# One-hot matrices kept in bf16 for the later layers of a graph network, with changes to its first and last steps

## The chip, the cores and the metric

One core of a Trainium2 chip runs the whole kernel. Its engines have an instruction stream each: TensorE (PE in the profile, its weight loads PEld) multiplies matrices, VectorE (DVE) and ScalarE (ACT) work on elements, GpSimd (POOL) issues the gathers, SyncE (SP) issues plain DMAs. All DMAs share 16 DMA engines. The metric is the device time of one execution in microseconds (us). Three runs of the kernel before gave 2895.53, 2903.81 and 2903.98 us, a median of 2903.81 us.

## The reference, cut to what matters

There are n = 6250 nodes with D = 256 features and 100000 edges, sorted by their target `dst`. `src` is random, and each edge has one of three relation types and 32 attributes.

```
ew = edge_attr @ edge_w + edge_b                    # one weight row per edge
rel_masks = [(edge_type == i) for i in range(3)]
inv_cnt = [1 / max(segment_sum(m, dst, n), 1) for m in rel_masks]
for l in range(3):
    msg = relu(x[src] * ew)
    out = sum over i of (segment_sum(msg * rel_masks[i], dst, n) * inv_cnt[i]) @ weights[l, i]
    x = x + relu(out + x @ roots[l] + biases[l])
result = layernorm(x_input + x)
```

## The kernel before, in words

**Tiles, pairs, quads and steps.** 128 edges are a tile, two tiles a pair, two pairs a quad; there are 782 tiles, 391 pairs and 196 quads. A layer is a loop over steps `it`, and at step `it` the pair `order[it]` is reduced. The parts of a pair's work stand in the same loop at different distances ahead of the reduction: the gather 9 steps ahead (`AHEAD`), the edge weights 6 to 4, the weighing 3, the one-hots 2. Every engine takes its instructions in the order in which this loop writes them (a manual schedule), and what one engine needs of another it waits for by semaphore. The planner (`order_of`, `spans_of`, `stages`, `schedule`) works out in which order the pairs come, which pairs form a span (pairs whose targets lie within 40 neighbouring nodes), at which step a span's sums are added, and at which step a block of 128 nodes is finished (`starts`). Layer 0 has 391 steps, layers 1 and 2 have 414 each.

**One pair.** `gather_pair` (L1378) has POOL fetch 128 rows of x for each tile, by an indirect DMA; the rows of a quad go to one of `ROWS` = 8 buffers `xs`. In layer 0 PE makes the edge weights out of the attributes and `ew_sb` (`make_ew`, L811 for the bias and L815), ACT copies them to `keep` (`keep_ew`, L771), and SP stores them in `ew_all` (L772). In layers 1 and 2 SP loads them again (`load_ew`, L759) and ACT copies them to PSUM (`seed_ew`, L786). DVE multiplies the rows by them (`weigh`, L838), ACT applies the relu (L839). `one_hot` makes the matrix that says which node of the window, and which relation, an edge belongs to: on DVE four `tensor_scalar` a quad (L852, one a tile, 128 x 120 in float32), in all three layers; in layer 0 ACT also writes a bf16 copy `oh_b` (L855), used to count edges. PE multiplies rows and one-hot (`reduce`, L870 and L878) into PSUM, for a span of several pairs the sums are turned (`take`, `turn`), and DVE adds them to `acc` (`add`, L918).

**The zone.** The first 52 pairs (few nodes, many edges) are gathered in layer 0 only: their rows are sorted by source class (`sort_hot`, `sort_count` with L628 to L632) and scattered by POOL to `zone_table` (`scatter`, L733) once their weights are in `keep`. Layers 1 and 2 load them in 39 lots (`load_ew`, L754) and make their one-hots from what was loaded.

**Nodes.** `node_mul` (L947, PE) multiplies a block's sums by the weights, `node_end` (DVE, L978 and L981) scales, adds and applies the relu, and SP stores the block in `x_mid` (L984). A block `c` has `node_mul` part 0 at step `starts[c]`, `node_end` part 0 and `node_mul` part 1 two steps later, `node_end` part 1 and the store four steps later; `clear` then empties its place in `acc`. In layer 2 `deviate` and `norm` follow.

**From layer to layer.** The next layer's first six pairs (12 gathers, `gather_early`) are fetched from all of `x_mid` but node block 1, so POOL waits at the first of them for the last store of the other 48 blocks. Block 1 is finished last of all; the gathers of the seventh pair on read the whole of `x_mid` and need its store too.

**The beginning.** The first part (`look`) reads `dst`, finds windows and sets `flag`; behind it a branch opens `ordered_path`, which loads `edge_w` and `edge_b` (L490 to L498), splits the bias into three bf16 parts (L505 to L511), zeroes `acc` in three large writes (L524 to L529), and stores a row block of zeros in each `x_mid` (L534). Then layer 0 begins. At step 20 of layer 0 `find_rows` and `find_came` prepare the indices of the later layers.

Of the kernel before, what the change touches and what calls it, by code (L numbers as in the profile page):

```python
# [442 lines left out]
def ordered_path(ctx, tc, x, attr_laid, A, weights, roots, biases, edge_w, edge_b, out, src, src_i, seg, place_i, consts, x_root,  # L443
# [7 lines left out]
    P = 128  # L451
# [30 lines left out]
    ew_all = [dram.tile([P, 4 * D], F32, name=f"ew_all{q}") for q in range(-(-U // 2))]  # L482
    table = dram.tile([(classes + 2 * Z) * P, D + 2], F32, name="zone_table")
# [4 lines left out]
    ew_sb = early_pool.tile([P, 2, D], F32, name="ew_sb")  # L488
    nc.vector.memset(ew_sb, 0.0)
    for j in range(OCT):  # L490
        nc.scalar.dma_start(ew_sb[j * A:(j + 1) * A, j % 2, :], edge_w)
    seed = early_pool.tile([P, D], F32, name="seed")
    nc.scalar.dma_start(seed, edge_b[None, :].to_broadcast([P, D]))
    blank = early_pool.tile([P, D + 2], F32, name="blank")
    bias = blank.bitcast(BF)[:PARTS, :2 * D].rearrange("p (i d) -> p i d", i=2)
    with tc.tile_pool(name="bias_s", bufs=1) as bias_s:
        left = bias_s.tile([P, D], F32, name="left")
        nc.scalar.dma_start(left, edge_b[None, :].to_broadcast([P, D]))  # L498
        row = bias_s.tile([P, 1], F32, name="row")
        nc.vector.tensor_copy(row, node_i)  # L500
        is_row = bias_s.tile([P, PARTS], F32, name="is_row")
        part = bias_s.tile([P, D], BF, name="part")
        rows_of = bias_s.tile([P, D], F32, name="rows_of")
        nc.vector.memset(rows_of, 0.0)
        for k in range(PARTS):  # L505
            nc.vector.tensor_scalar(is_row[:, k:k + 1], row, float(k), None, op0=ALU.is_equal)
            nc.vector.tensor_copy(part, left)
            nc.vector.tensor_sub(left, left, part)
            nc.vector.scalar_tensor_tensor(rows_of, part, is_row[:, k:k + 1], rows_of, op0=ALU.mult, op1=ALU.add)
        for i in range(2):  # L510
            nc.vector.tensor_copy(bias[:, i, :], rows_of[:PARTS, :])  # L511

# [20 lines left out]
    for rows_of in x_mid:  # L533
        nc.scalar.dma_start(rows_of[N - P:N, :], x_all[:, NT - 1, :])  # L534
# [47 lines left out]
    hots = {}  # L582
# [41 lines left out]
    def sort_count(g):  # L624
        n, t = len(tiles_in(g)), 3 * g
        seat = o_pool.tile([P, 2, D], F32, name="o_p")
        flat = seat.rearrange("p a d -> p (a d)")[:, :n * classes]
        nc.tensor.matmul(flat, before, hots[g][:, :n].rearrange("p t w -> p (t w)"), start=True, stop=False)  # L628
        nc.tensor.matmul(flat, full_ones, total[:, :n].rearrange("p t w -> p (t w)"), start=False, stop=True)
        nc.vector.tensor_mul(hots[g][:, :n], flat.rearrange("p (t w) -> p t w", w=classes), hots[g][:, :n])  # L630
# [23 lines left out]
    def sort_step(it):  # L654
# [30 lines left out]
    def layer(l, r_sb, b_sb, ats, early, pools):  # L685
# [6 lines left out]
        soon = min(SOON, steps - max(starts[:1] + starts[2:]) - 5)  # L692
# [10 lines left out]
        at_qs = {}  # L703
# [143 lines left out]
        def one_hot(q):  # L847
# [5 lines left out]
            if l == 0:  # L853
                oh_bs[q] = early_pool.tile([P, 4, WK], BF, name="oh_b", bufs=2)
                nc.scalar.activation(oh_bs[q][:, :n], ohs[q][:, :n], AF.Copy)  # L855
# [710 lines left out]
```

## Time and profile before

| | |
|---|---|
| median of three runs | 2903.81 us (2895.53 to 2903.98) |
| the profiled execution, its own time | 2903.96 us |
| its span, first to last instruction | 2902.2 us |
| mean granted TensorE clock | 0.948 |
| first gather begins | 4.04 us |
| first gather for layer 1 begins | 1159.06 us |
| first gather for layer 2 begins | 2017.61 us |
| last gather begins | 2882.09 us |
| DMA traffic | 668.25 MB, mean 230 GB/s |

How to read its rows: in a timeline each row has the start and the duration in us, engine, line, operation, what is written and read, and in brackets how long the engine had been idle before and what released it ("issue" is time in which the engine waited for nothing that the profile shows). A group's row has the count, busy us and the mean ns of one, then the idle time before. A row of waits has the sum in us, the number of times and the longest. A row of windows has the stretch and, for each engine, the busy us and the number of instructions.

### The profile page before, as it was taken

The numbers are of one execution on the slowest core, as the hardware profiler recorded it, in microseconds if no ns is written. First come the engines' busy times: TensorE is split into PE (matmuls) and PEld (weight loads), VectorE is DVE, ScalarE is ACT, GpSimd is POOL, SyncE is SP. The second block draws the span as 40 slices with busy tenths as digits, with TensorE's granted clock in tenths as the row PEclk, the third lists the DMA queues.
The fourth block names the chain that finished last, engine by engine and source line by source line (L and its number), as shares of the span: only waits on it lengthen the run. The fifth ranks groups of instructions, "written<-read, shape, count | busy, mean of one in ns | idle before, by whom it ended". The sixth has DMA issues, their size and how long they took to land. (4 is left out here: it accounts for less than half of the span.)

```text
span 2902.2 us, 44132 instructions
## 1 busy us (share of the span) xinstructions
PE 2409.1 (83%) x13302; PEld 1880.6 (65%) x13302; DVE 2207.5 (76%) x5612; ACT 1708.1 (59%) x2220; POOL 2138.6 (74%) x2253
## 2 busy tenths in 40 slices
PE   5799988888988789788898888777888888878776
PEld 2466656555666566577777777665666767767665
DVE  7777766766656576677878888776788888888986
ACT  5677766666666667455655555444555555555654
POOL 7676777777777775777777777776777777767775
PEclk9899998999889999999999999898999999999998
DMA  7898665556555666887777777676777777777765
GB/s 237 280 328 272 207 198 190 189 185 196 185 192 187 196 211 202 267 262 240 256 242 243 246 237 257 215 223 195 269 255 262 255 256 240 244 227 233 249 227 156
DMA packets 285411, 668.25 MB, mean 230 GB/s; under 512 B 50555, under 2 KB 142509, under 8 KB 285165
## 3 DMA queue, kind: packets, MB, share of 16 engines
q1 hardware_dynamic: 170112, 362.98, 35.9%
q0 software_dynamic: 107616, 294.11, 33.9%
q10 hardware_dynamic: 7436, 8.24, 0.9%
q8 instruction: 110, 1.80, 0.3%
q14 instruction: 137, 1.11, 0.1%
HBM read 528.50 MB, written 136.63 MB: 229 GB/s over the span
## 5 line engine op out<-in xcount | busy, mean ns | idle before, releaser
L1378 POOL DMA_INDIRECT xs<-x_mid,src_r x1332 | 1265.3, 950 | 420.1 <-issue 343.1
L1378 POOL DMA_INDIRECT xs<-in_x_dram,src_io x770 | 734.9, 954 | 243.1 <-issue 211.8
L839 ACT ACTIVATE xs<-xs 128x1024 f32<-128x1024 f32 x533 | 559.5, 1050 | 582.8 <-DVE xs L838 561.0
L838 DVE TENSOR_TENSOR xs<-ew_p,xs 128x1024 f32<-128x1024 f32 x533 | 646.5, 1213 | 314.3 <-ACT keep L771 176.3
L878 PE MATMUL h_p<-oh,xs 128*128 128x120 f32 x4768 | 692.5, 293 | 202.7 <-DVE acc L918 105.4
L878 PEld LDWEIGHTS h_p<-oh,xs 128*128 128x128 f32 x4768 | 641.3, 203 | 304.9 <-DVE acc L918 112.4
L852 DVE TENSOR_SCALAR oh<-iota_w,seg_o 128x120 f32<-128x120 f32 x2138 | 568.2, 328 | 0.0
L870 PE MATMUL h_p<-xs,oh 128*120 128x256 f32 x1868 | 517.7, 405 | 41.5 <-issue 14.7
L947 PE MATMUL o_p<-w_sb,acc 128*128 128x256 f32 (+1 forms) x1752 | 456.1, 397 | 64.8 <-DVE x_root L978 56.6
L918 DVE TENSOR_TENSOR acc<-h_p,acc 128x240 f32 (+1 forms) x764 | 338.9, 445 | 113.5 <-PE o_p L947 45.7
L947 PEld LDWEIGHTS o_p<-w_sb,acc 128*128 128x128 f32 (+1 forms) x1752 | 323.6, 195 | 141.5 <-DVE x_root L978 73.9
L870 PEld LDWEIGHTS h_p<-xs,oh 128*120 128x120 f32 x1868 | 319.5, 189 | 146.6 <-issue 30.0
L786 ACT ACTIVATE ew_p<-ew_s 128x1024 f32<-128x1024 f32 (+1 forms) x340 | 343.3, 1010 | 12.7 <-DMA ew_s<-ew_all 12.7
L771 ACT ACTIVATE keep<-ew_p 128x1024 f32<-128x1024 f32 x170 | 173.2, 1019 | 226.1 <-issue 115.5
L978 DVE SCALAR_TENSOR_TENSOR x_root<-o_p,inv,x_root 128x256 f32<-128x256 f32 (+1 forms) x438 | 210.5, 480 | 43.0 <-PE o_p L947 36.1
L839 ACT ACTIVATE zone<-zone 128x1024 f32<-128x1024 f32 (+1 forms) x78 | 78.8, 1010 | 223.9 <-DVE zone L838 223.9
L815 PE MATMUL ew_p<-ew_sb,at 64*128 64x512 f32 x630 | 199.0, 710 | 11.8 <-ACT ew_p L789 11.7
L789 ACT ACTIVATE ew_p<-seed 128x1024 f32<-128x1024 f32 (+1 forms) x194 | 198.5, 1023 | 0.0
L931 PE MATMUL r_p<-r_sb,t_s 128*128 128x256 f32 x588 | 158.7, 392 | 21.7 <-ACT t_s L927 21.4
L838 DVE TENSOR_TENSOR zone<-ew_p,zone 128x1024 f32<-128x1024 f32 (+1 forms) x78 | 90.6, 1162 | 107.5 <-PE ew_p L801 107.3
L870 PE MATMUL h_p<-zone,oh 128*120 128x256 f32 x576 | 148.0, 387 | 11.6 <-DVE acc L918 7.0
L801 PE MATMUL ew_p<-x_all,hot 128*128 128x256 f32 x588 | 150.6, 401 | 7.6 <-DVE hot L794 7.4
(178 smaller groups left out, 2340.8 us busy)
## 6 DMA issues: line engine op xcount, KB each, us to landing
ew_s<-ew_all SPq DMA_DIRECT2D x338, 512.0 KB
ew_all<-keep SPq DMA_DIRECT2D x169, 512.0 KB
zone<-zone_table SPq DMA_DIRECT2D x72, 516.0 KB
xs<-x_mid,src_r POOLq DMA_INDIRECT x1332
zone_table<-blank SPq DMA_DIRECT2D x21, 677.2 KB
xs<-in_x_dram,src_io POOLq DMA_INDIRECT x770
x_mid<-x_all SPq DMA_DIRECT2D x96, 128.0 KB
at<-in_attr_laid_dram SPq DMA_DIRECT2D x40, 256.0 KB
```

The costliest lines, as they stand in the source:

```text
L786: nc.scalar.activation(ew_ps[q][:, :n], ew_ss[q][:, :n], AF.Copy)
L789: nc.scalar.activation(ew_ps[q][:, :n], seed[:, None, None, :].to_broadcast([P, n, 2, D]), AF.Copy)
L815: nc.tensor.matmul(ew_ps[q][:, k].rearrange("p i d -> p (i d)"), at[half, :], ew_sb[half].rearrange("p i d -> p (i d)"), start=False, stop ...
L838: nc.vector.tensor_mul(there, ew_ps[q][:, pairs.start:pairs.stop, :n], there)
L839: nc.scalar.activation(there, there, AF.Relu)
L852: nc.vector.tensor_scalar(ohs[q][:, i, :], iota_w[:, :, :WIN], at, None, op0=ALU.is_equal)
L870: nc.tensor.matmul(h_p[:WK, :D], ohs[u // 2][:, t, :], rows_of(u, i), start=(i == 0 and first), stop=(i == n - 1 and closes(u)), skip_grou ...
L878: nc.tensor.matmul(h_p[:, d * WK:(d + 1) * WK], rows_of(u, i)[:, d * P:(d + 1) * P] if d < DC else full_ones, (ohs if d < DC else oh_bs)[u ...
L918: nc.vector.tensor_tensor(there, h_ps[span][:, :CH * WK].rearrange("p (c r w) -> p c r w", c=CH, r=R), there, op=ALU.add)
L947: nc.tensor.matmul(o_p[:n, j, :], acc[:, d, r, slot:slot + n], w_sb[:, r * DC + d, :], start=(d == 0), stop=(d == DC - 1))
L978: nc.vector.scalar_tensor_tensor(root, o_p[:n, j, :], inv[:n, c, r:r + 1], root, op0=ALU.mult, op1=ALU.add)
L1378: nc.gpsimd.indirect_dma_start(out=xs[:, u % 2, i, :], out_offset=None, in_=x_rows[:, :], in_offset=bass.IndirectOffsetOnAxis(ap=src_i[:, ...
```

## The change

- **One-hots.** In layer 0 SP stores each regular quad's bf16 one-hots (`oh_b`, now three buffers) in a new DRAM tensor `oh_all`, 128 rows of 960 bytes. In layers 1 and 2 SP loads them six steps ahead (`load_oh`, three buffers), and ACT widens them to float32 in one instruction a quad, in the place of the four DVE instructions. The zone's lots keep theirs.
- **The sort.** What DVE does with the counts (`sort_rank`) moves one step behind the PE multiplications (`sort_count`), and the sorting steps may lie one step closer to the node steps.
- **The beginning.** `edge_b` and `edge_w` are loaded ahead of the look instead of behind the branch, into four places of `x_root` (`staged`; `ROOTS` is 21, and layer 0 uses 17); the bias is split at the end of the look. The copies of window bases in the look are grouped by equal span length: 16 in place of 54. `acc` is zeroed by ACT alone: 256 columns before layer 0, the rest in nine pieces at steps 0, 2, ... 16. The zero rows of `x_mid` are stored by SP instead of ACT.
- **The last steps.** The last five blocks (`QUICK`) have their parts one step apart in place of two; their starts in layer 0 become 366, 369, 372, 375, 378 (before: 366, 370, 374, 378, 382), in layers 1 and 2 388, 392, 396, 399, 402 (before: 388, 393, 397, 401, 405). The span that ends with the last pair is added as soon as it is summed, and the very last span has five pairs in place of seven. The number of steps and the start of block 1 stay.

```
+    oh_all = [dram.tile([P, 4 * WK], BF, name=f"oh_all{q}") for q in range(-(-U // 2))]
...
+    ew_sb, bias, seed = staged(x_root)
...
-    for c in range(DC + 1):
-        if c < DC // 2:
-            nc.vector.memset(acc[:, c], 0.0)
-        else:
-            nc.scalar.activation(acc[:, c].rearrange("p r n -> p (r n)"),
-                                 zero.to_broadcast([P, R * (ASIDE + 2 * P + WIN)]), AF.Copy)
+    def zero_acc(n0, n1):
+        nc.scalar.activation(acc[:, :, :, n0:n1], zero[:, :, None, None].to_broadcast([P, DC + 1, R, n1 - n0]), AF.Copy)
+
+    zero_acc(P, 3 * P)
+    zero_at = {0: (3 * P, 4 * P), 2: (ASIDE, ASIDE + P), 4: (ASIDE + P, ASIDE + 2 * P + WIN), 6: (4 * P, 5 * P),
+               8: (5 * P, 6 * P), 10: (6 * P, 7 * P), 12: (7 * P, 8 * P), 14: (0, P), 16: (RING, ASIDE)}
...
     for rows_of in x_mid:
-        nc.scalar.dma_start(rows_of[N - P:N, :], x_all[:, NT - 1, :])
+        nc.sync.dma_start(rows_of[N - P:N, :], x_all[:, NT - 1, :])
...
-                           if not any(s - 1 <= p <= s + 4 for s in taken_by)))
+                           if not any(s <= p <= s + 4 for s in taken_by)))
...
+    def sort_rank(g):
+        n, t = len(tiles_in(g)), 3 * g
+        flat = seats[g].rearrange("p a d -> p (a d)")[:, :n * classes]
         nc.vector.tensor_mul(hots[g][:, :n], flat.rearrange("p (t w) -> p t w", w=classes), hots[g][:, :n])
...
         if it in sort_at[:-1]:
             sort_count(sort_at.index(it))
+        if it - 1 in sort_at[:-1]:
+            sort_rank(sort_at.index(it - 1))
...
+        def load_oh(q):
+            n = tiles_of(q)
+            oh_ls[q] = late_pool.tile([P, 4, WK], BF, name="oh_l", bufs=3)
+            nc.sync.dma_start(oh_ls[q][:, :n].rearrange("p t w -> p (t w)"), oh_all[q][:, :n * WK])
...
         def one_hot(q):
             ohs[q] = edge.tile([P, 4, WK], F32, name="oh", bufs=3)
             n = tiles_of(q)
+            if q in oh_ls:
+                nc.scalar.activation(ohs[q][:, :n], oh_ls[q][:, :n], AF.Copy)
+                return
...
-                oh_bs[q] = early_pool.tile([P, 4, WK], BF, name="oh_b", bufs=2)
+                oh_bs[q] = early_pool.tile([P, 4, WK], BF, name="oh_b", bufs=3)
                 nc.scalar.activation(oh_bs[q][:, :n], ohs[q][:, :n], AF.Copy)
+                if 2 * q >= Z:
+                    nc.sync.dma_start(oh_all[q][:, :n * WK], oh_bs[q][:, :n].rearrange("p t w -> p (t w)"))
...
+        next_at = {s + paces(c, NT): c for s, c in node_at.items()}
+        over_at = {s + 2 * paces(c, NT): c for s, c in node_at.items()}
...
+            if l > 0 and pair(LOAD_OH) is not None and first_of(it + LOAD_OH, 2) and pair(LOAD_OH) < ZU:
+                load_oh(pair(LOAD_OH) // 2)
             if l > 0 and pair(LOAD_EW) is not None and first_of(it + LOAD_EW, 2):
                 load_ew(pair(LOAD_EW) // 2)
...
+            if l == 0 and it in zero_at:
+                zero_acc(*zero_at[it])
...
-            if it - 2 in node_at:
-                node_end(node_at[it - 2], 0)
-            if it - 4 in node_at:
-                node_end(node_at[it - 4], 1)
+            if it in next_at:
+                node_end(next_at[it], 0)
+            if it in over_at:
+                node_end(over_at[it], 1)
...
-    stops = {K, last, middle, *quads, *lots}
+    stops = {K, last, last + 5, middle, *quads, *lots}
...
+        if spans[group[-1]][1] == -(-E // 256):
+            by = 0
         by = max(by, done + 1 + some)
...
+def paces(c, NT):
+
+    return 1 if c >= NT - QUICK else 2
...
-        step = starts[c] = max(done[c] + 2, step + 4)
+        step = starts[c] = max(done[c] + paces(c, NT), step + 2 + paces(max(c - 1, 2), NT))
...
+def staged(x_root):
+    D = x_root.shape[2]
+    first = ROOTS - STAGED
+    return (x_root[:, first:first + 2, :],
+            x_root.bitcast(BF)[:PARTS, first + 2, :].rearrange("p (i d) -> p i d", i=2),
+            x_root[:, first + 3, :])
...
+        ew_sb, bias, seed = staged(x_root)
+        A = edge_w.shape[0]
+        nc.scalar.dma_start(seed, edge_b[None, :].to_broadcast([P, D]))
+        nc.vector.memset(ew_sb, 0.0)
+        for j in range(OCT):
+            nc.scalar.dma_start(ew_sb[j * A:(j + 1) * A, j % 2, :], edge_w)
...
+        left = look.tile([P, D], F32, name="left")
+        is_row = look.tile([P, PARTS], F32, name="is_row")
+        part = look.tile([P, D], BF, name="part")
+        rows_of = look.tile([P, D], F32, name="rows_of")
+        for k in range(PARTS):
+            rest_of = left if k else seed
```

More of the change, by code (lines that the diff above doesn't have):

```diff
@@ L487, in ordered_path @@
     early_pool = only.enter_context(tc.tile_pool(name="first", bufs=1, side="right"))
[L488 to L493, printed above, removed]
-    blank = early_pool.tile([P, D + 2], F32, name="blank")
[L495 to L511, printed above, removed]
+    ew_sb, bias, seed = staged(x_root)
+    blank = early_pool.tile([P, D + 2], F32, name="blank")
     x_all = big.tile([P, NT, D], F32, name="x_all")
@@ L691, in layer @@
         steps = len(order)
-        soon = min(SOON, steps - max(starts[:1] + starts[2:]) - 5)
+        soon = min(SOON, steps - starts[0] - 5, *(steps - starts[c] - 2 * paces(c, NT) - 1 for c in range(2, NT)))
         taken, turns, added, banks = stages(N, E, share, l)
@@ L1459 @@
             nc.vector.tensor_scalar(limits[:, 0, last:clear], limits[:, 0, last:clear], float(P), None, op0=ALU.max)
+        runs = []
         for u, v in spans_of(N, E)[Z // 2:]:
-            if v > u + 1:
-                nc.vector.tensor_copy(base_g[:, u + 1:v], base[:, u:u + 1].to_broadcast([1, v - u - 1]))
+            if runs and runs[-1][1] == v - u:
+                runs[-1][2] += 1
+            else:
+                runs.append([u, v - u, 1])
+        for u, n, k in runs:
+            if n > 1:
+                there = base_g[:, u:u + n * k].rearrange("p (k n) -> p k n", n=n)
+                first = base[:, u:u + n * k].rearrange("p (k n) -> p k n", n=n)[:, :, 0:1]
+                nc.vector.tensor_copy(there[:, :, 1:], first.to_broadcast([1, k, n - 1]))
         base_p = look_p.tile([P, 512], F32, name="base_p", bufs=1)
```

49 lines of the change are left out of this document (31 added, 18 removed).

## The prediction

> **What bounds the kernel now.** I read the page first, then the groups by line, then POOL's timeline from end to end, and last the waits and windows of the stretches where POOL stops. No engine is full on the page, and the busiest, PE and DVE, suggest that moving DVE's work is worth much:
>
> ```profile
> span 2902.2 us, 44132 instructions
> PE 2409.1 (83%) x13302; PEld 1880.6 (65%) x13302; DVE 2207.5 (76%) x5612; ACT 1708.1 (59%) x2220; POOL 2138.6 (74%) x2253
> q1 hardware_dynamic: 170112, 362.98, 35.9%
> ```
>
> POOL's 74% misleads. Its groups of gathers and scatters:
>
> ```profile
> L1378 POOL DMA_INDIRECT xs<-x_mid,src_r x1332 | 1265.3, 950 | 420.1 <-issue 343.1 <-DMA xs<-x_mid,src_r 15.2 <-ACT xs L839 12.6
> L1378 POOL DMA_INDIRECT xs<-in_x_dram,src_io x770 | 734.9, 954 | 243.1 <-issue 211.8 <-DMA xs<-in_x_dram,src_io 6.1 <-PE ew_p L815 5.2
> L733 POOL DMA_INDIRECT zone_table<-keep,slot_i x104 | 101.9, 980 | 42.9 <-issue 25.9 <-ACT keep L765 11.5 <-DMA xs<-in_x_dram,src_io 2.7
> ```
>
> A gather is busy for 0.95 us, and the timeline puts 0.30 us of "issue" behind each, so one takes 1.25 us and a pair 2.5 us. With the 36 gathers that open the layers these are 2242, about 2802 us of a span of 2902. POOL's timeline has only these larger holes:
>
> ```profile
> 4.04 1.11 POOL L1378 DMA_INDIRECT x_root<-in_x_dram,src_f  x1 [1.67 <-DMA src_f<-in_src_laid_dram]
> ...
> 94.16 0.95 POOL L1378 DMA_INDIRECT xs<-in_x_dram,src_io  x1 [0.30 <-issue]
> ...
> 105.04 0.94 POOL L1378 DMA_INDIRECT xs<-in_x_dram,src_io  x1 [7.43 <-issue]
> ...
> 293.82 1.00 POOL L733 DMA_INDIRECT zone_table<-keep,slot_i  x1 [11.48 <-ACT keep L765]
> ...
> 1159.06 0.94 POOL L1378 DMA_INDIRECT xs<-x_mid,src_e  x1 [16.81 <-DMA x_mid<-x_all]
> ...
> 1174.06 0.94 POOL L1378 DMA_INDIRECT xs<-x_mid,src_r  x1 [0.30 <-issue]
> ...
> 2017.61 0.95 POOL L1378 DMA_INDIRECT xs<-x_mid,src_e  x1 [9.23 <-issue]
> ...
> 2450.54 0.94 POOL L1378 DMA_INDIRECT xs<-x_mid,src_r  x1 [1.03 <-issue]
> ...
> 2619.78 1.11 POOL L1378 DMA_INDIRECT xs<-x_mid,src_r  x1 [2.27 <-ACT xs L839]
> ...
> 2882.09 0.95 POOL L1378 DMA_INDIRECT xs<-x_mid,src_r  x1 [0.30 <-issue]
> ```
>
> Beyond the usual 0.30 us they are: 7.1 us at 105; 11.2 at 294; 16.5 at 1159; 8.9 at 2018; twelve between 2450 and 2620 (first and last shown) with 14.3 in sum; three small ones before 290 with 1.5. Together 59.5 us. Everything else is gathers, the first 4.0 us, and 20.1 us from the last gather's start to the end. So POOL sets the pace nearly everywhere, and I count only what the change does to these holes and to the two ends. Cheaper DVE work where POOL does not stop is worth nothing.
>
> **The first stretch, to 294 us.** Here the steps run behind POOL, and POOL stops at 105 because its eight buffers are full and at 294 because the first scatter needs weights that ACT has not yet copied. If the steps come d earlier at 294, POOL goes on d earlier, up to the 19.8 us of the five holes. Four edits move d:
>
> ```profile
> 30.94 1.01 PE L811 MATMUL ew_p<-blank,full_ones 3*128 3x512 bf16 x2 [14.67 <-DVE blank L511]
> 0.74 0.40 SPq L1425 DMA_DIRECT2D src_f<-in_src_laid_dram  x1
> 18.83 3.67 SPq L563 DMA_DIRECT2D at<-in_attr_laid_dram  x2
> 5.88 3.54 DVE L1462 COPY base_g<-base 1x5 f32<-1x5 f32 x54
> 20.49 0.48 DVE L489 MEMSET ew_sb<- 128x512 f32 x1
> 26.71 0.29 DVE L507 CAST part<-left 128x256 bf16<-128x256 f32 x1 [0.90 <-DMA left<-in_L_gnn_edge_b_dram]
> 30.35 0.54 DVE L511 CAST blank<-rows_of 3x256 bf16<-3x256 f32 x2
> 1114.38 1.15 ACT L964 ACTIVATE acc<-zero_o 128x1152 f32<-128x1152 f32 x1
> 145.10:217.60 72.50, 67.53 (x359) 45.31 (x359) 56.78 (x152) 54.90 (x74) 54.45 (x58) 1.00 0.97 328
> DVE sort_hot L630 <- PE o_p L629: 13.0, 11, 3.0
> ```
>
> (1) PE's first edge weights wait for the bias until 30.94. With the bias split ahead of the branch only DVE's `full_ones` is left. DVE passed the branch at 20.49; the look gains the bias work (first and last row: 26.71 to 30.89, 4.2 us) and a 0.48 us zeroing, and loses some 2.5 of the 3.54 us of copies (16 in place of 54), so `full_ones` is there at about 23. But SP now stands in a wait: the two zero rows of `x_mid` need DVE's zeroing at about 23.5, and behind them in SP's queue lie `r_sb`, `b_sb` and the attributes, which were issued at 18.83 and will be at about 25. From issue to landing the first index load shows 3.3 us (0.74 to the gather at 4.04), so the attributes are there at 28 to 29 and the first weights 3 us sooner than before; bounds -1 (SP's stores slow) and 8 (30.94 less 23). (2) `acc` is zeroed in nine pieces between steps 0 and 16: seven of 128 x 1152 at 1.15 us, one 1.3 times and one a third of that, 10 us of ACT in the first 40 us of steps, where two large writes used to stand ahead of the steps. ACT has gaps there, but keeps order with DVE: I take 3 us lost, bounds 0 and 10. (3) `sort_rank` one step later ends the 13.0 us that DVE waited for PE between 110 and 294. PE, busy 67.5 of 72.5 us, gives back at most its own idle 7%, 13 us of 184; I take 5, bounds 0 and 13. (4) 123 KB of one-hots a quad are stored, on DMA engines that the last window row shows busy 0.97. At the page's q1, 35.9% of 2902 us for 363 MB or 2.9 us a MB, that is 0.35 us a quad. POOL is eight quads, 40 us, ahead of the reduction at 105, and at 294 still so far that it must stand for 11.48 us until the steps have come up; that lead covers later landings, and I take nothing; without it, 0.35 us for each of some 23 quads would be 8 us. So d = 3 - 3 + 5 = 5 us; the bounds are -19 and the 19.8 of the holes.
>
> **Between layers 0 and 1.** POOL waits for the store of block 48; then come 12 gathers, and at 1174.06 the first that needs block 1:
>
> ```profile
> 1153.91 0.43 DVE L981 SCALAR_TENSOR_TENSOR x_all<-x_root,x_all 106x256 f32<-106x256 f32 x1
> 1164.13 0.42 DVE L981 SCALAR_TENSOR_TENSOR x_all<-x_root,x_all 128x256 f32<-128x256 f32 x1
> 2012.20 0.43 DVE L981 SCALAR_TENSOR_TENSOR x_all<-x_root,x_all 106x256 f32<-106x256 f32 x1
> 2020.39 0.42 DVE L981 SCALAR_TENSOR_TENSOR x_all<-x_root,x_all 128x256 f32<-128x256 f32 x1
> ```
>
> Block 48 ended at step 386 and will at 380. Six steps of 2.5 us are 15 us, less some crowding, so its store no longer holds POOL long after 1145. But block 1 stays the last: its rows were ready at 1164.55, and from 1154.34 to 1159.06 block 48's store took 4.7 us to release POOL, so block 1's frees the gathers at about 1169.2. The wait removed is replaced by a shorter one in front of the thirteenth gather: of 16.5 us, 1174.06 - 1169.2 = 5 us are won. Bounds 3 (crowded last blocks delay block 1) and 8 (block 48's PE work is out of the way).
>
> **Between layers 1 and 2.** Block 48 is ready five steps or 12 us earlier, before POOL asks, so the 8.9 us go; twelve gathers then end at 2023.7, and block 1's rows, ready at 2020.81, land at 2025.5 at the same 4.7 us. A little over 1 us of new wait, 7.5 won; bounds 5 and 8.9.
>
> **Layer 2 from 2450 to 2620.** There the steps themselves are too slow and POOL fills its buffers:
>
> ```profile
> 2394.15:2466.70 72.55, 59.45 (x385) 52.32 (x386) 63.15 (x164) 39.84 (x52) 53.45 (x58) 1.00 0.73 240
> 2611.80:2684.30 72.50, 60.15 (x378) 53.68 (x377) 64.59 (x174) 42.33 (x58) 53.48 (x57) 0.95 0.74 233
> L852 DVE TENSOR_SCALAR oh<-iota_w,seg_o 128x120 f32<-128x120 f32 x1352 | 359.1, 328 | 0.0
> L855 ACT ACTIVATE oh_b<-oh 128x480 bf16<-128x480 f32 x195 | 116.3, 596 | 25.5 <-DVE oh L852 25.3
> ACT ew_p L786 <- DMA ew_s<-ew_all: 12.7, 5, 5.3
> SPq L984 <- DVE x_all L981: 354.6, 66, 14.8
> ```
>
> DVE (third engine in a window row) has 63 to 65 us of 72.5. The 1352 one-hots of layers 1 and 2 held it for 359.1 us, 0.266 each net (328 ns with their overlap); 58 in a window are 15.4 us, which leaves 49, below PE's 60 and well below POOL's pace. ACT takes up the widening. No row shows bf16 to float32; the reverse over the same 128 x 480 takes 0.596 us, and 480 columns should lie between 480/1152 of the zeroing's 1.15 us, 0.48, and the whole 1.15. I take the 0.6 of the nearest row, 8.7 us a window: ACT rises from 42 to 51 (at 1.15 to 59, still no bound). Of the 14.3 us I count 13 won; bounds 9 and 14.3. The loads add 0.35 us of DMA to each 5 us, at a share of 0.74: no bound. They have four steps, 10 us, from SP's issue to ACT's use, as the edge weights have, for which ACT waited 12.7 us in all. Elsewhere in layers 1 and 2 POOL does not stop, and these 359 us buy nothing.
>
> **The end.** The last gather's rows are weighed behind four one-hots:
>
> ```profile
> 2885.69 1.04 DVE L852 TENSOR_SCALAR oh<-iota_w,seg_o 128x120 f32<-128x120 f32 x4
> ```
>
> Those go to ACT and block 48 is out of the way, but the landing of the gather bounds what is left: 1 us won, bounds -1 and 2.
>
> **A rule to weigh against this.** While DVE stood idle for 8 us, gathers at 94.16 and around it took 0.95 + 0.30 us, as they do beside a busy DVE:
>
> ```profile
> 97.79 2.44 DVE L683 TENSOR_SCALAR came<-came,next_i 128x128 f32<-128x128 int32 x12 [8.17 <-DMA came<-in_src_dram]
> ```
>
> The Trainium skill, "SBUF — State Buffer", section "SBUF: two separate sides", says that a VectorE operation in a two-port mode locks GpSimd out of the port over which it writes its DMA descriptors; by it the one-hots' departure would speed up every gather of layers 1 and 2. The trace speaks against it: 0.94 us is the shortest gather and 0.950 the mean of 1332, so the most that it could be worth is 13 us.
>
> **Sum.** 5 + 5 + 7.5 + 13 + 1 = 31.5 us off the profiled execution's 2903.96 us (span 2902.2 and 1.8 around it), which stands within 0.2 us of the median: 2872.5 us.
>
> **Rivals.** *A, the beginning falls back* (10 in 100): SP's wait and ACT's zeroing push the steps 10 us later, so the hole at 294 grows to 21. For it: ACT and DMA are nearly full there. Against it: 13 us of waits go. 2904 + 10 - 26.5 = 2887.5 us, still faster; in half of this case the other terms shrink as well, and the change is below 8.7 us, the 0.3% that a measurement of this kernel can tell from nothing. *B, slower* (7 in 100): a one-hot lands too late. SP takes its queue in order and waits up to 14.8 us in front of an `x_mid` store, with `load_oh` behind it; ACT then stands at the widening with the relu and the weights of the next quads behind it, and DVE and PE after that. It decides when a quad takes over 5 us again and again. Half a microsecond at each of the 96 blocks stored in layers 1 and 2 is 48 us: 2904 + 48 - 31.5 = 2920 us. Against it: the four steps of lead. *C, the port* (7 in 100): POOL's own pace improves, by the 13 us above, to 2859.5 us. *That nothing moves* (2 in 100): the holes of layer 2 are PE's and the boundary waits only change their names: 2895 us and more.
>
> **How the numbers follow.** The forecast has 74 in 100. Its terms at their worst together would give 2907, at their best 2851; all at one end is unlikely, so I take 2856 to 2892, which holds A's 2887.5 and C's 2859.5. Faster by over 0.3%: 74 + 7 + half of A, 86. Slower: 7. Within: 7.
>
> **What would show it.** Right: gathers still 1.25 us apart; no hole between 2450 and 2620; the first gather for layer 1 right behind the last of layer 0 and a new hole in front of the thirteenth; DVE some 350 us and ACT's busy time some 200 us changed. Wrong: a hole at 294 larger than 11.5 us, ACT waiting for `oh_l`, or POOL at another pace.

## The result, and the profile after

The changed kernel takes 2875.71 us (median of four, 2872.09 to 2877.39), the kernel before 2901.26 us (median of four): a ratio of 0.991, interval 0.9895 to 0.9929. In a later set of runs it was 2877.52 against 2903.31 us, ratio 0.990 (0.989 to 0.992). Three of the four sets of experiments fell on chips on which the kernel before itself takes 3904 to 3970 us (why, as far as it is seen, stands in the last section), so from those sets only ratios within the set, and what the trace shows of single events, are read.

The page of the profiled execution (2872.09 us of its own):

```profile
span 2870.1 us, 44287 instructions
PE 2388.6 (83%) x13286; PEld 1875.6 (65%) x13286; DVE 1887.4 (66%) x4216; ACT 1876.6 (65%) x2571; POOL 2137.1 (74%) x2253
q1 hardware_dynamic: 243840, 425.76, 43.1%
L1397 POOL DMA_INDIRECT xs<-x_mid,src_r x1332 | 1264.2, 949 | 408.9 <-issue 338.5
L844 DVE TENSOR_SCALAR oh<-iota_w,seg_o 128x120 f32<-128x120 f32 x782 | 208.0, 328 | 0.0
L840 ACT ACTIVATE oh<-oh_l 128x480 f32<-128x480 bf16 (+1 forms) x340 | 200.3, 589 | 0.0
```

DVE is busy 320 us less, ACT 168 us more, and 63 MB more go through q1, the queue of the plain DMAs. The span fell by a tenth of what DVE lost: 32.1 us. A gather takes 949 ns as before (950). ACT's widening takes 589 ns (0.6 us in the prediction) and has no idle time in front of it, so ACT never stood waiting for the load of a one-hot.

All of POOL's holes over 0.45 us, in its timeline from end to end, and the first and the last gather:

```profile
3.97 1.10 POOL L1397 DMA_INDIRECT x_root<-in_x_dram,src_f  x1 [1.61 <-DMA src_f<-in_src_laid_dram]
...
105.67 0.94 POOL L1397 DMA_INDIRECT xs<-in_x_dram,src_io  x1 [9.66 <-ACT xs L828]
...
287.67 1.00 POOL L717 DMA_INDIRECT zone_table<-keep,slot_i  x1 [5.76 <-ACT keep L754]
...
1147.78 0.94 POOL L1397 DMA_INDIRECT xs<-x_mid,src_e  x1 [11.10 <-DMA r_sb<-in_L_gnn_roots_dram]
...
1165.83 0.95 POOL L1397 DMA_INDIRECT xs<-x_mid,src_r  x1 [3.34 <-PE r_p L819]
...
2849.77 0.95 POOL L1397 DMA_INDIRECT xs<-x_mid,src_r  x1 [0.30 <-issue]
```

The holes at 2018 and between 2450 and 2620 are gone, the one at 288 is half as large, the one between the layers, now at 1148, is smaller and has a second one behind it in front of the thirteenth gather. Only the one at 105 grew (9.66 us, 7.43 before). In layer 2 the windows that stood beside these holes now have DVE (third engine) less busy than PE (first):

```profile
2394.15:2466.70 72.55, 61.28 (x402) 54.40 (x401) 54.87 (x120) 50.16 (x72) 55.09 (x58) 1.00 0.84 279
2611.80:2684.30 72.50, 59.59 (x379) 52.64 (x377) 52.00 (x118) 50.81 (x75) 54.81 (x59) 0.95 0.85 275
```

DVE went from 63 and 65 us to 55 and 52, ACT from 40 and 42 to 50 and 51, DMA's share from 0.73 and 0.74 to 0.84 and 0.85.

### The profile page after: what moved, and what is told of

Read it like the earlier page. It is cut to its first block, busy times and chain, and to the rows that moved or that the text cites. A ratio compares the mean times of both kernels' runs of the same rounds, so it can differ in the third digit from the quotient of the medians.

```text
span 2870.1 us, 44287 instructions
## 1 busy us (share of the span) xinstructions
PE 2388.6 (83%) x13286; PEld 1875.6 (65%) x13286; DVE 1887.4 (66%) x4216; ACT 1876.6 (65%) x2571; POOL 2137.1 (74%) x2253
## 4 chain that ended last, share of the span: by engine, by line
PE 17%; POOL 9%; DMA 9%; issue 8%; DVE 6%; ACT 3%; DVEq 0%; SPq 0%; ACTq 0%; POOLq 0%
POOL xs L1397 9%; DMA xs<-x_mid,src_r 8%; PE h_p L864 4%; PE h_p L872 4%; PE o_p L941 4%; DVE xs L827 2%; PE ew_p L790 2%; PE r_p L925 1%; ACT xs L828 1%; DVE x_root L972 1%; ACT ew_p L775 1%; DVE acc L912 1%; DVE oh L844 1%; PE h_p L884 0%; DMA oh_l<-oh_all 0%
## 5 line engine op out<-in xcount | busy, mean ns | idle before, releaser
L872 PE MATMUL h_p<-oh,xs 128*128 128x120 f32 x4720 | 683.0, 292 | 195.4 <-DVE acc L912 116.4
L872 PEld LDWEIGHTS h_p<-oh,xs 128*128 128x128 f32 x4720 | 634.8, 202 | 291.6 <-DVE acc L912 122.5
L804 PE MATMUL ew_p<-x_root,at 64*128 64x512 f32 x630 | 199.1, 710 | 26.9 <-ACT ew_p L778 14.2
L844 DVE TENSOR_SCALAR oh<-iota_w,seg_o 128x120 f32<-128x120 f32 x782 | 208.0, 328 | 0.0
L840 ACT ACTIVATE oh<-oh_l 128x480 f32<-128x480 bf16 (+1 forms) x340 | 200.3, 589 | 0.0
L778 ACT ACTIVATE ew_p<-x_root 128x1024 f32<-128x1024 f32 (+1 forms) x194 | 198.3, 1022 | 0.0
L958 ACT ACTIVATE acc<-zero_o 128x768 f32<-128x768 f32 (+1 forms) x150 | 140.8, 938 | 29.2 <-PE o_p L941 25.9
## 6 DMA issues: line engine op xcount, KB each, us to landing
x_mid<-x_all SPq DMA_DIRECT2D x98, 128.0 KB
```

Source lines behind the costliest of these rows:

```text
L804: nc.tensor.matmul(ew_ps[q][:, k].rearrange("p i d -> p (i d)"), at[half, :], ew_sb[half].rearrange("p i d -> p (i d)"), start=False, stop ...
L840: nc.scalar.activation(ohs[q][:, :n], oh_ls[q][:, :n], AF.Copy)
L844: nc.vector.tensor_scalar(ohs[q][:, i, :], iota_w[:, :, :WIN], at, None, op0=ALU.is_equal)
L872: nc.tensor.matmul(h_p[:, d * WK:(d + 1) * WK], rows_of(u, i)[:, d * P:(d + 1) * P] if d < DC else full_ones, (ohs if d < DC else oh_bs)[u ...
```

## The experiments

**The theory** is that of the prediction: POOL's gathers set the time, and each part of the change is worth what it takes off POOL's holes. **The rival** is that 350 us less work on DVE are worth something by themselves. Four kernels ran on a chip where the kernel before takes 2903.31 us.

**control**: the changed kernel itself.

> The changed kernel itself once more, as the measure for the others of this call. Where the kernel before takes 2900 us: 2872 to 2878 us again, ratio 0.991. On a chip like the two on which the earlier experiments ran (kernel before 3900 to 3970 us, TensorE standing still for 4 to 17 us again and again): if POOL's holes were what the change removed and TensorE sets the time there, most of it is worth nothing there, ratio 0.995 to 1.000; if the change takes work off whatever is the bound, 0.991 as before.

2877.52 us, ratio 0.990 (0.989 to 0.992). Its profiled execution, 2882.28 us, was the slowest of its four, 10.2 us above the execution shown above. Holes in layer 2 that the latter did not have are 8.1 us of that:

```profile
2564.60 0.94 POOL L1397 DMA_INDIRECT xs<-x_mid,src_r  x1 [0.69 <-issue]
...
2581.28 0.95 POOL L1397 DMA_INDIRECT xs<-x_mid,src_r  x1 [6.99 <-ACT oh L840]
...
2597.45 1.10 POOL L1397 DMA_INDIRECT xs<-x_mid,src_r  x1 [1.34 <-ACT xs L828]
```

ACT is named as the one that released POOL at 2581.28, but its widenings before that had not waited for a load. DVE waited for PE, and PE once for DVE, around the blocks:

```profile
2563.01 0.41 DVE L912 TENSOR_TENSOR acc<-h_p,acc 128x240 f32 x1 [4.49 <-PE o_p L941]
...
2570.11 2.03 PE L864 MATMUL h_p<-zone,oh 128*120 128x256 f32 x4 [2.75 <-DVE acc L912]
```

Ahead of this, PE stands still for 3.38 us with "issue" as the reason, up to 2546.02 here and up to 2540.05 in the execution above. The 10 us behind that pause, first in the control and then above (the number behind the five engines is the granted TensorE clock):

```profile
2546.00:2556.00 10.00, 9.23 (x41) 8.60 (x42) 2.85 (x8) 2.51 (x5) 7.56 (x9) 0.52 0.49 140
```

```profile
2540.00:2550.00 10.00, 7.20 (x54) 6.54 (x55) 5.33 (x11) 4.48 (x8) 7.56 (x9) 1.00 0.63 180
```

In the control the clock was 0.52, and PE was busy for 9.23 us with 41 matmuls; in the execution without holes in layer 2 it was 1.00, and PE did 54 in 7.20 us. The profiled executions of quick_late and all3 below have the same pause, a clock of 0.54 and 0.52 behind it, and holes in layer 2 as well. So over four executions these holes go with the clock behind the pause; that it causes them was not tried, and their sizes (8.1, 1.0 and 2.6 us) do not follow it.

**oh_only**: the kernel before with the one-hot part alone (the loader, its three buffers and `LOAD_OH` = 6 as in the change).

```
+                if 2 * q >= Z:
+                    nc.sync.dma_start(oh_all[q][:, :n * WK], oh_bs[q][:, :n].rearrange("p t w -> p (t w)"))
...
+            if q in oh_ls:
+                nc.scalar.activation(ohs[q][:, :n], oh_ls[q][:, :n], AF.Copy)
+                return
...
-ROOTS = 22
+ROOTS = 21
```

> The kernel before with the one-hot part alone (stored in bf16 in layer 0, loaded and widened by ScalarE in layers 1 and 2, ROOTS 21 for the space). Theory: only the holes of layer 2 between 2450 and 2620 go, 13 to 14 us: 2887 us where the kernel before takes 2901; on a chip where TensorE sets the time, nothing, ratio 0.998 to 1.002. Rival (taking 350 us off VectorE is worth more than the holes): 2880 us or less, ratio under 0.993, on either kind of chip.

2896.05 us, ratio 0.998 (0.997 to 0.999): faster by 7 us, half of what the theory said, and far from the rival's 2880. Yet it takes 314 us off DVE, nearly all of the 320 that the whole change takes:

```profile
PE 2393.0 (83%) x13302; PEld 1878.2 (65%) x13302; DVE 1893.5 (65%) x4256; ACT 1871.0 (65%) x2560; POOL 2138.3 (74%) x2253
```

Its POOL timeline tells where the two halves of the theory's gain are:

```profile
106.16 0.94 POOL L1392 DMA_INDIRECT xs<-in_x_dram,src_io  x1 [9.55 <-issue]
...
296.28 0.99 POOL L734 DMA_INDIRECT zone_table<-keep,slot_i  x1 [11.48 <-ACT keep L771]
...
1164.01 0.94 POOL L1392 DMA_INDIRECT xs<-x_mid,src_e  x1 [18.95 <-PE h_p L889]
...
2020.94 0.96 POOL L1392 DMA_INDIRECT xs<-x_mid,src_e  x1 [7.81 <-PE h_p L889]
...
2871.32 0.95 POOL L1392 DMA_INDIRECT xs<-x_mid,src_r  x1 [0.30 <-issue]
```

Behind 2020.94 no hole is left: in this execution the one-hot part alone removes all 14.3 us of layer 2. But layer 0 is slower than in the profile before. The 52nd quad (counted from 0) is weighed at 305.35 us (302.89 before), the 188th at 1122.43 (1117.73), and the holes before 300 and between the layers are 3.1 and 2.1 us larger. That is little more than two executions of one kernel differ by: in the changed kernel and in the control, which are the same, these quads are weighed at 297.16 and 298.99 us, at 1114.58 and 1117.62. Layer 0 differs in the store of 123 KB a quad, which uses the two buffers of `oh_b` too (the change has three), and in the one place less in `x_root`; whether any of these costs the 5 us was not tried.

**quick_late**: the last five blocks one step apart in layers 1 and 2 only.

```
-def paces(c, NT):
+def paces(c, NT, l):
-    return 1 if c >= NT - QUICK else 2
+    return 1 if l > 0 and c >= NT - QUICK else 2
```

> Changed kernel with the last five blocks of layer 0 two steps apart again, one step in layers 1 and 2 only. Theory (in layer 0 the early last blocks crowd the steps before the end, so that block 1 comes only 1.2 us sooner): block 1's rows are ready 3 to 4 us sooner, but block 48's rows come later by 8 to 10 us and hold the first gather for layer 1: the same time within 3 us, 2874 to 2879 us. Rival (the crowding costs more than the blocks' earlier end brings): 2868 to 2872 us. On a chip where TensorE sets the time: equal to the changed kernel within 0.3%.

2882.20 us, ratio 0.992 (0.991 to 0.994), 4.7 us above the control and above the 2874 to 2879 us of the theory, though the interval overlaps the control's. The end of layer 0, DVE's rows of blocks 48 and 1 and POOL's first gathers for layers 1 and 2 that had to wait:

```profile
1148.99 0.42 DVE L975 SCALAR_TENSOR_TENSOR x_all<-x_root,x_all 106x256 f32<-106x256 f32 x1
1159.58 0.42 DVE L975 SCALAR_TENSOR_TENSOR x_all<-x_root,x_all 128x256 f32<-128x256 f32 x1
...
1154.17 0.94 POOL L1397 DMA_INDIRECT xs<-x_mid,src_e  x1 [16.96 <-DMA oh_all<-oh_b]
...
2019.33 0.95 POOL L1397 DMA_INDIRECT xs<-x_mid,src_r  x1 [1.12 <-DMA x_mid<-x_all]
```

The same two blocks in the changed kernel:

```profile
1141.54 0.43 DVE L975 SCALAR_TENSOR_TENSOR x_all<-x_root,x_all 106x256 f32<-106x256 f32 x1
...
1162.91 0.43 DVE L975 SCALAR_TENSOR_TENSOR x_all<-x_root,x_all 128x256 f32<-128x256 f32 x1
```

Both halves of the theory are seen. With two steps between them block 1 comes 3.3 us sooner and block 48 7.5 us later. Block 1's sooner end brings nothing then, since block 48 alone holds POOL: 16.7 us beyond the usual 0.30, where the changed kernel has 13.8 in two holes. So quick blocks win 2.8 us of holes in layer 0. Counted from the end of layer 0's last gather, block 1's rows are ready after 22.3 us in the kernel before, 22.8 here and 26.7 in the changed kernel: that the quick blocks crowd block 1 by about 4 us is shown.

**all3**: quick_late with two edits to the beginning.

```
-        nc.sync.dma_start(rows_of[N - P:N, :], x_all[:, NT - 1, :])
+        nc.scalar.dma_start(rows_of[N - P:N, :], x_all[:, NT - 1, :])
...
-            if l == 0 and it == 20:
+            if l == 0 and it == 2:
                 find_rows()
                 find_came()
+            if l == 0 and it == 20:
+                mark_came()
```

(`mark_came` is the comparison that stood at the end of `find_came`.)

> Changed kernel with the zero rows of x_mid stored from ScalarE's queue, the sources looked up at step 2 in place of 20, and the quick last blocks in layers 1 and 2 only: the candidate that should beat both. Theory: POOL's holes at 105 and 288 go to under 2 us, the boundary of layers 0 and 1 unchanged: 2860 to 2864 us, ratio 0.986. Rival (TensorE or ScalarE eats the sooner start): 2870 to 2876 us. On a chip where TensorE sets the time: 0.2 to 0.5% below the changed kernel, by the stand of TensorE at the start alone.

2867.63 us, ratio 0.987 (0.986 to 0.989): 9.9 us below the control, 14.6 below quick_late, from which only the two edits to the beginning part it, and faster than both kernels. Its holes before 300 are 1.4 us in all; the largest:

```profile
112.23 0.94 POOL L1401 DMA_INDIRECT xs<-in_x_dram,src_io  x1 [0.65 <-ACT ew_p L780]
...
275.03 0.99 POOL L719 DMA_INDIRECT zone_table<-keep,slot_i  x1 [1.08 <-ACT keep L756]
...
1141.23 0.94 POOL L1401 DMA_INDIRECT xs<-x_mid,src_e  x1 [16.65 <-DMA oh_all<-oh_b]
```

The first weighing, the comparison of `came` and the weighing of the 12th quad in the changed kernel, and behind them in this one:

```profile
33.35 1.23 DVE L827 TENSOR_TENSOR x_root<-ew_p,x_root 128x1024 f32<-128x1024 f32 x1 [11.60 <-ACT keep L760]
...
98.42 2.44 DVE L667 TENSOR_SCALAR came<-came,next_i 128x128 f32<-128x128 int32 x12 [9.15 <-DMA came<-in_src_dram]
...
103.20 1.21 DVE L827 TENSOR_TENSOR xs<-ew_p,xs 128x1024 f32<-128x1024 f32 x1
```

```profile
26.08 1.22 DVE L829 TENSOR_TENSOR x_root<-ew_p,x_root 128x1024 f32<-128x1024 f32 x1 [4.40 <-ACT keep L762]
...
81.91 2.43 DVE L669 TENSOR_SCALAR came<-came,next_i 128x128 f32<-128x128 int32 x12
...
86.82 1.22 DVE L829 TENSOR_TENSOR xs<-ew_p,xs 128x1024 f32<-128x1024 f32 x1
```

The steps start 7.3 us sooner, of which 3.8 are left at the 11th quad (80.77 against 84.52), and then do not stand 9 us at step 20: the 12th quad is weighed at 86.82 us in place of 103.20. The holes before 300 lose 13 us (14.4 in quick_late, 1.4 here), as the theory had it. The median is 4 us above the theory's 2860 to 2864 all the same: layer 2 has holes of 2.6 us in this execution. It also has 2.2 us more behind the last gather's start than the changed kernel's (22.5 and 20.3).

**The sum over six executions.** POOL's idle time beyond 0.30 us, in holes over 0.45 us, by stretch:

| kernel | before 300 | layers 0 to 1 | layers 1 to 2 | layer 2 | all | own time | own time less all |
|---|---|---|---|---|---|---|---|
| before | 19.8 | 16.5 | 8.9 | 14.3 | 59.5 | 2903.96 | 2844.5 |
| oh_only | 22.9 | 18.6 | 7.5 | 0 | 49.0 | 2894.38 | 2845.4 |
| control | 15.4 | 13.9 | 0 | 8.1 | 37.4 | 2882.28 | 2844.9 |
| quick_late | 14.4 | 16.7 | 0.8 | 1.0 | 33.0 | 2878.44 | 2845.5 |
| changed | 14.8 | 13.8 | 0 | 0 | 28.7 | 2872.09 | 2843.4 |
| all3 | 1.4 | 16.4 | 0 | 2.6 | 20.3 | 2867.69 | 2847.4 |

The last column is each profiled execution's own time without its holes. It stays within 4 us while the time moves by 36: in these executions the differences are in POOL's holes. The column alone does not decide between theory and rival. POOL issues the same gathers in every kernel, so its time less its holes has to be nearly constant, and the same subtraction leaves 2850 to 2869 us on the other chips too, where POOL has about 1000 to 1100 us of holes and waits for the other engines everywhere. What decides is how few the holes are here (20 to 60 us, in 4 to 19 places), and oh_only: 314 us less work on DVE closed holes of 14 us and moved the median by 7. The table also says that layer 2's holes come and go from one execution to the next.

**The sets on the other chips.** Each expects times as on the first chip, so what can be held against them is a ratio within a set and a row.

**no_sort** and, in another set, **no_sort_2**: the ranking back in the step of its PE multiplications.

```
-        if it - 1 in sort_at[:-1]:
-            sort_rank(sort_at.index(it - 1))
+            sort_rank(sort_at.index(it))
```

> The kernel after, with the ranks of the sort taken in the same step as the counts. By the holes: DVE waits for PE again in the sorting steps, the hole at the first scatter grows from 5.8 to about 11 us, everything later moves by 5: 2881 us. If PE sets the pace of the steps there anyway: the hole stays at 6 us and the time at 2876.

> The changed kernel with the sort's ranking back in the step of its PE multiplications. Theory (DVE's wait of 29 us in all for these multiplications, 13 of it before 294, made the early steps late): DVE waits some 13 us for them before 290 again, the 52nd quad is weighed at 302 us in place of 297 to 299, and the holes before 290 grow by 5 us to 20: 2881 to 2883 us, ratio 0.993. Rival (DVE's time in that wait was waited for elsewhere anyway): the 52nd quad at 297 to 299, holes of 15 us, 2876 to 2878 us.

Ratios 0.996 (0.992 to 1.000) and 1.000 (0.997 to 1.002); beside them stood 0.991 for sp_free and 0.989 for both_2, which leave the ranking where the change put it. DVE's wait for the counts, first in no_sort and then in sp_free:

```profile
L612 DVE TENSOR_TENSOR sort_hot<-o_p,sort_hot 128x441 bf16<-128x441 f32 x34 | 21.1, 620 | 102.3 <-remote 66.7 <-PE o_p L607 25.8 <-PE h_p L885 3.2
```

```profile
L612 DVE TENSOR_TENSOR sort_hot<-o_p,sort_hot 128x441 bf16<-128x441 f32 x34 | 20.9, 613 | 24.5 <-PE ew_p L804 14.2 <-remote 5.1 <-PE h_p L867 3.1
```

The 52nd quad is weighed at 392.2 and 391.6 us without the move, at 373.5 to 385.6 in the other kernels of those sets, in which that wait is 20 to 27 us. So on those chips the wait is not paid elsewhere anyway, and there half or all of the change's gain goes with the move (the theory's ratio was 0.993). The changed kernel itself did not run beside them, and on the chips where it was forecast the move's 5 us were not measured by taking it away.

**sp_free**: the changed kernel with the zero rows of `x_mid` on ScalarE's queue (the first two lines of all3's diff).

> The kernel after, with the zero rows of x_mid stored by ACT's queue again, so that SP issues the attributes right behind the branch. By the prediction's step on SP's queue: the attributes land about 6 us sooner, the first edge weights are made at 24 in place of 30.1 us, the hole at the first scatter closes (5.8 us) or nearly so: 2870 us. If ACT's zeroing or the DMA engines set the pace of the first steps: the steps have lost the 6 us again by 100 us, and the time stays at 2876.

Ratio 0.991 (0.988 to 0.994). The first weighing comes at 27.54 us, in the kernels of that set with the rows on SP's queue at 33.26 to 34.73: the place on SP's queue costs 6 to 7 us at the start, as all3 shows as well. At the 12th quad 1.3 to 5.7 us of that are left (126.7 us, 128.0 to 132.4 in the others), so whether the hole at the first scatter closes by this alone stays open.

**no_oh**, **no_oh_2** and **no_quick**: without the one-hot part, and with all blocks two steps apart.

```
-                if 2 * q >= Z:
-                    nc.sync.dma_start(oh_all[q][:, :n * WK], oh_bs[q][:, :n].rearrange("p t w -> p (t w)"))
...
-            if l > 0 and pair(LOAD_OH) is not None and first_of(it + LOAD_OH, 2) and pair(LOAD_OH) < ZU:
-                load_oh(pair(LOAD_OH) // 2)
```

> The kernel after, with the one-hots of layers 1 and 2 made by DVE again (neither stored nor loaded). By the holes in POOL's row: the gathers keep 0.95 + 0.30 us, the holes between 2420 and 2590 come back with about 14 us in sum, the rest stays; some 14 us more than after, 2890 us. By the port between DVE and POOL: no holes, but the mean of the 1332 gathers above 0.949 us, up to 13 us in all. By DVE's work itself (300 us more in layers 1 and 2 than after): 30 us and more.

> Changed kernel with DVE making the one-hots in all layers again (no store, no load, nothing for ScalarE to widen). Theory (in layer 2 DVE's one-hots made the steps slower than the gathers): the holes in POOL's row between 2420 and 2600 come back with about 14 us in sum, DVE's busy share of a 72.5 us stretch there is 62 to 65 us in place of 54, nothing else moves: some 2890 us where the changed kernel takes 2876. Rival (these holes were the crowded sums and blocks of PE, and went with the other edits): holes under 3 us in sum, 2876 to 2879 us.

```
-QUICK = 5
+QUICK = 0
...
-    stops = {K, last, last + 5, middle, *quads, *lots}
+    stops = {K, last, middle, *quads, *lots}
...
-        if spans[group[-1]][1] == -(-E // 256):
-            by = 0
```

> The kernel after, with the last steps as before (five last blocks two steps apart, last span of seven pairs, the last pair's span added late). By the holes: the first gather for layer 2 waits its 8.9 us again, and layers 0 and 1 are again joined by one hole of 16 to 19 us in place of 11.1 + 3.3: 11 to 12 us more than after, 2887 us. By crowding as the main effect (the steps of layer 0 lost about 5 us near 1115 against the kernel before): block 1 of layer 0 is ready earlier, and only 4 to 8 us are lost, 2881 us.

Ratios 0.991 (0.987 to 0.996), 0.994 (0.991 to 0.997) and 0.992 (0.987 to 0.996). On those chips taking either part out is not told from leaving both in (0.991 in sp_free, 0.994 in both). POOL there waits for the other engines everywhere (880 us of idle time before the gathers of layers 1 and 2 in no_sort, 409 in the profile above), so the times say nothing about the holes, and the theory of no_oh (14 us) was not tested. One event can be read: in no_quick a single hole of 36.3 us stands in front of layer 1's first gather, and in sp_free two, of 17.6 us there and of 13.2 us in front of the thirteenth. That is the joining that was expected of no_quick.

**both** and **both_2**: all3 with quick blocks in layer 0 too, to see whether the two add up.

> Changed kernel with two more edits to its beginning: the zero rows of x_mid are stored from ScalarE's queue again, so that nothing on SyncE's queue stands in front of the attributes; and the sources for find_came are loaded and looked up at step 2 in place of step 20, only their comparison stays at step 20. Theory (the steps of layer 0 start late and lose time at step 20, and POOL has to wait for them at 105 and 288): first attributes land 2 to 3 us sooner, no 8 us wait of DVE for the load at step 20, POOL's holes at 105 and 288 (9.4 and 5.5 us beyond the usual 0.30) shrink to under 2 us together: 2861 to 2864 us. Rival (PE or ScalarE sets the pace of the first 290 us, a sooner start is lost again there): the holes keep over 8 us in sum, 2868 to 2874 us.

> The candidate once more, with the quick last blocks in all three layers: the changed kernel with the zero rows of x_mid stored from ScalarE's queue and the sources looked up at step 2. In the run with quick blocks in layers 1 and 2 only, POOL's holes before 290 had gone from 14.7 us to 2.7, and the hole between layers 0 and 1 was 16.4 us, 13.9 in the changed kernel. Theory (the two add up): holes of 3 us before 290 and 14 between the layers, 2.5 us below the 2867.6 of that run: 2865 us where the kernel before takes 2903. Rival (steps that come sooner crowd the end of layer 0 as much as the quick blocks clear it): 16 us or more between the layers, 2867 to 2870 us.

Ratios 0.994 (0.992 to 0.997) and 0.989 (0.986 to 0.993), both on chips of the other kind. DVE's wait for `came` at step 20 is gone there as well. Between the layers POOL waits 20.8 and 13.1 us in both, 20.5 and 12.9 in both_2, but all3 did not run on those chips, so whether this is the better candidate stays open.

## Why the prediction was right, point by point

Forecast 2872.5 us in 2856 to 2892, measured 2875.7. Between the two profiled executions 31.9 us went, and 31.5 had been forecast; between the medians 25.6, and between the profiles before and of the control 21.7. That the first pair meets the sum so closely is luck: terms were off by up to 2.3 us in both directions, and the execution was the fastest of its four, without a hole in layer 2. The table of the six executions gives each term:

- **What bounds the kernel** was right: POOL's pace (949 to 950 ns a gather of layers 1 and 2 in these six executions) and its holes.
- **The first stretch**, 5 forecast, 5.0 and 4.4 measured, with parts that were off in both directions. The attributes were issued at 23.29 us, sooner than the 25 assumed, but landed at 30.09, 6.8 us later and not 3.3: the first weighing moved 1.7 us and not 3. At the 11th quad 0.3 us of that were left (84.52 us, 84.84 before), a loss of 1.4 where 3 had been allowed for ACT's zeroing; what took them was not separated. Between the 11th and the 52nd quad 5.4 us were won (3.5 in the control), where the sort was given 5 and the one-hot store nothing. DVE's wait for the sort's counts before 300 fell from 13.2 us to 0.6. But no run on such a chip takes the move away, so what it won and what the store cost are not told apart; oh_only only hints that the store is not free.

```profile
23.29 1.43 SPq L541 DMA_DIRECT2D at<-in_attr_laid_dram  x2
...
30.09 2.17 PE L804 MATMUL ew_p<-x_root,at 64*128 64x512 f32 x4 [7.40 <-DMA at<-in_attr_laid_dram]
```

- What was not seen: the row of `came`, which the prediction quotes to show POOL beside an idle DVE, is itself a stall of the steps, by 8 to 11 us at step 20. All3 shows that it and the place on SP's queue together hold nearly all that is left before 300.
- **Layers 0 to 1**, 5 forecast, 2.7 measured, below the lower bound of 3. The sum was taken at the right place, the thirteenth gather, which waits for block 1; a hole in front of it came as forecast. But block 48 still holds POOL: the first gather for layer 1 does not stand right behind the last of layer 0, the sign that the prediction named, but behind a hole of 10.8 us beyond the 0.30, most of the 13.8. Block 48's row ends at 1141.97 and the first gather begins 5.8 us later (4.7 before), though the profile names a load issued right behind the store. Counted from the last gather of layer 0, that row came 6.8 us sooner and not 15. Block 1's rows came 4.4 us later, counted in the same way, where the sum took them as unmoved; that is the crowding that quick_late shows. The gathers were released 2.5 us after these rows and not 4.7, which gave back 2.2 of that.
- **Layers 1 to 2**, 7.5 forecast, 8.9 measured; oh_only, with the old pace, keeps 7.5 of that hole. The new wait of a little over 1 us (1.8 by the prediction's own 2025.5 and 2023.7, which leaves 7.1) is seen in quick_late (0.8 beyond 0.30) and not in the changed kernel.
- **Layer 2**, 13 forecast: 14.3 in the first execution and in oh_only, 13.3 in quick_late, 11.7 in all3, 6.2 in the control. DVE is no longer the bound there (55 and 52 us in the windows, where the prediction left 49), but the steps can still fall behind POOL, in the three executions in which the clock was low behind PE's pause.
- **The end**, 1 forecast, nothing measured: 20.3 us from the last gather's start, 20.1 before (21.1 to 22.5 in the other four executions). The last row's weighing waits for the gather, which the prediction gave as the bound.

```profile
2854.56 0.42 DVE L833 TENSOR_TENSOR xs<-ew_p,xs 128x256 f32<-128x256 f32 x1 [2.66 <-DMA xs<-x_mid,src_r]
```

The other signs came: gathers 1.25 us apart, no hole between 2450 and 2620 (in this execution), DVE 320 us less and ACT 168 more, where some 350 and 200 were named. Of the rivals, A and B are refuted: the hole at 288 shrank, and no widening waits for its load; that nothing moves is refuted by the time. C, the port rule of the Trainium skill ("SBUF — State Buffer", section "SBUF: two separate sides"), is refuted as a price: over 1350 one-hots left DVE, and the gathers of layers 1 and 2 went from 950 to 949 ns. Whether those one-hots ran in a two-port mode, no run here shows.

## What to carry to other kernels

Find the engine whose instructions follow one another at a constant distance, list its holes, and price an edit only by the holes that it can close: here 314 us off one engine closed holes of 14, and two edits at the start holes of 13. Before pricing an edit that starts something sooner, follow the next wait behind it (here `came`), since an earlier gain is lost there. Blocks that end sooner crowd the block that ends last. And one profile is one execution: the same kernel had no hole in layer 2 in one and 8.1 us in another, so compare a forecast with several.

## What the runs showed of the hardware

On three other chips the kernel before takes 3904 to 3970 us. The gathers' own duration is the same there (951 ns in no_sort), but PE stands still again and again: behind 300 us, pauses of over 4 us with "issue" as the reason come once or twice in each of the six executions of the table (5.4 us at most), and 18 to 33 times in each of the eight profiles from those chips (up to 19.7 us). In no_sort, windows of 4 us in layer 2, and rows of PE's and DVE's timelines in them:

```profile
2500.00:2504.00 4.00, 2.06 (x12) 1.67 (x11) 0.00 (x0) 0.00 (x0) 2.85 (x3) 1.00 0.72 243
2504.00:2508.00 4.00, 0.26 (x1) 0.19 (x1) 0.00 (x0) 0.00 (x0) 1.90 (x2) 0.84 0.34 98
2508.00:2512.00 4.00, 0.00 (x0) 0.00 (x0) 3.46 (x8) 2.96 (x4) 2.03 (x3) 0.50 0.12 33
2512.00:2516.00 4.00, 3.63 (x16) 3.57 (x17) 3.16 (x7) 3.15 (x5) 2.62 (x3) 0.50 0.80 215
```

```profile
2505.63 0.26 PE L871 MATMUL h_p<-oh,xs 128*128 128x120 f32 x1 [1.64 <-issue]
2512.37 2.03 PE L871 MATMUL h_p<-oh,xs 128*128 128x120 f32 x8 [6.48 <-issue]
...
2508.47 0.42 DVE L826 TENSOR_TENSOR zone<-ew_p,zone 128x256 f32<-128x256 f32 x1 [11.13 <-remote]
```

PE works at a fraction of its pace from 2501 and not at all from 2506 to 2512, waiting for nothing that the profile shows. DVE and ACT have stood still since 2497.3 and 2498.9, ahead of PE, and work again from 2508.5, before PE does; what DVE waited for the profile does not name ("remote"). So the trace does not show which engine stops the others. The clock granted falls from 1.00 to 0.50 only after PE's pause has begun. The Trainium skill, "TensorE: Matmul & The Clock Gate", section "What's actually happening", says that the clock is halved after an idle window; the trace agrees, and by that rule the low mean clock of these runs (0.83) would be an effect of PE's standing idle and not its cause. On the chips where the kernel before takes 2900 us, one pause of 3.38 us in layer 2 was followed by a low clock in three executions and by 1.00 in a fourth (see control). What causes the pauses stays open.
